# Dividing the attention features by their denominator ahead of one joined product

## The chip, the cores and the metric

The kernel runs on one core of one Trainium2 chip. The metric is the device time of one execution in microseconds (us), lower is better. Its engines work side by side, each through its own queue in order: PE (TensorE, matrix products and transposes into PSUM), DVE (VectorE, elementwise work), ACT (ScalarE, functions of one operand), POOL (GpSimd), and SP (SyncE, which issues DMAs). They wait for one another through semaphores.

## The reference, cut to what matters

The model has four layers; the change is in the attention of the last one. It is a linear attention over the 4096 pixels of each of 4 images, with 128 channels in 8 heads of 16:

```python
def _L3_attn_ref(Q, Wq, bq, Wk, bk, Wv, bv, Wo, bo):
    q = (Q @ Wq + bq).reshape(bs, seq, N_HEADS, HEAD_DIM)
    k = (Q @ Wk + bk).reshape(bs, seq, N_HEADS, HEAD_DIM)
    v = (Q @ Wv + bv).reshape(bs, seq, N_HEADS, HEAD_DIM)
    phi_q = jax.nn.elu(q) + 1.0
    phi_k = jax.nn.elu(k) + 1.0
    KV = jnp.einsum('blhd,blhm->bhdm', phi_k, v)
    K_sum = phi_k.sum(axis=1)
    Z = 1.0 / (jnp.einsum('blhd,bhd->blh', phi_q, K_sum) + EPS)
    V_new = jnp.einsum('blhd,bhdm->blhm', phi_q, KV) * Z[..., None]
    out = V_new.reshape(bs, seq, N_HEADS * HEAD_DIM) @ Wo + bo
    return out
...
t = t + _L3_attn_ref(_ln_t(t), ...)
```

So for each pixel and head there is a vector of 16 features `phi_q`, a denominator (one number for the head), and a 16x16 matrix `KV` that is the same for all pixels of an image.

## The kernel before, in words

The four images stay in SBUF (`xs`, 128 channels by 4096 pixels each). `layer3_attention` goes over them in chunks of 512 pixels, 8 to an image. For each image there are two generators.

`summed(b)` has three steps to a chunk: `norm` (the layer norm: a centring product `ln_xc`, squares on ACT, their mean by a product `ln_var`, a transpose `ln_vt` and an addition `ln_sd` on DVE, the power -1/2 on POOL (L140), four transposes on PE (L129) that spread the result, and the product `nrm` on DVE), `keys` (the joined product `kv` with the key and value matrices, then the key's feature `e_k`), and `add`, which accumulates `kv_sum` over all pixels in one PSUM tile by four products per chunk. At the end of the image, DVE turns `kv_sum` into `kvh` (the matrix `KV` of all heads, zero outside the 16x16 blocks, by the mask `same16`) and `ksh` (the sums of the features, masked alike).

`answered(b)` has three steps to a chunk as well: `queries` (the product `q_ps`, and its feature `e_q` through ACT and DVE), `weighed` (the products `den_ps` with `ksh` and `num_ps` with `kvh`; `den_t`, `rd`, `z`: the denominator is turned by 32x32 blocks, cut to one column per head, inverted, turned back and spread over the head; then `vn`, numerator times inverse), and `give` (the product `o_ps` with the output projection `wo`, and the addition to the image, `x` in the profile).

`in_turn` staggers the steps of one generator, so that in one turn step three works on chunk c, step two on c+1 and step one on c+2. `run` takes two generators in turns: the sums of image b+1 go along with the answers of image b. So the layer has three stages: the sums of image 0 alone, three times sums and answers together (8 chunks each), and the answers of image 3 alone.

The order of the instructions in each engine's queue isn't written out in the code: the framework orders them when the kernel is built, from the program order and its own estimate of when each could start. So an edit of one step can move others in the queues. All products here take fp32 operands, and one product shows as two records in the trace. PSUM tiles of the tag "mm" rotate through 7 buffers; most SBUF work tiles have 2.

Of the kernel before, what the change touches and what calls it, by code (L numbers as in the profile page):

```python
# [9 lines left out]
F32 = mybir.dt.float32  # L10
# [3 lines left out]
ALU = mybir.AluOpType  # L14
# [3 lines left out]
P = 128  # L18
# [3 lines left out]
CH = 512  # L22
# [8 lines left out]
class Common:  # L31
# [59 lines left out]
    def mm(self, out, lhsT, rhs, start=True, stop=True):  # L91
        self.nc.tensor.matmul(out, lhsT, rhs, start=start, stop=stop)  # L92
# [165 lines left out]
def column(nc, pool, v, name, n=1, p=P):  # L258

    t = pool.tile([p, n], F32, name=name)  # L260
    nc.sync.dma_start(out=t, in_=v.rearrange("(n p) -> p n", p=p))
    return t


def matrix(nc, pool, m, name, k=1):

    rows, f = m.shape
    if k == 1:
        t = pool.tile([rows, f], F32, name=name)
        nc.sync.dma_start(out=t, in_=m)  # L270
    else:
        t = pool.tile([rows // k, k, f], F32, name=name)
        nc.sync.dma_start(out=t, in_=m.rearrange("(k p) f -> p k f", k=k))
    return t


def rows(nc, pool, v, name):

    t = pool.tile([P, v.shape[0]], F32, name=name)
    nc.sync.dma_start(out=t, in_=v.partition_broadcast(P))  # L280
    return t
# [812 lines left out]
def in_turn(n, *stages):  # L1094


    for i in range(n + len(stages) - 1):
        for k in reversed(range(len(stages))):
            if 0 <= i - k < n:
                stages[k](i - k)  # L1100
                yield
# [21 lines left out]
def run(*parts):  # L1123
    for _ in in_turns(*parts):
        pass
# [875 lines left out]
def layer3_attention(K, xs, w):  # L2001

    nc, tc, mm = K.nc, K.tc, K.mm
    HD = 16
    with ExitStack() as ctx:
        pool = lambda name, bufs, **kw: ctx.enter_context(tc.tile_pool(reuse_waits="tile", name=name, bufs=bufs, **kw))
        cst = pool("l3_const", 1)
        big = pool("l3_big", 2)
        work = pool("l3_work", 2)
        psum = pool("l3_ps", 7, space=PSUM)  # L2010
        pskv = pool("l3_pskv", 1, space=PSUM)

        wkv = cst.tile([P, 2 * P], F32, name="wkv")
        nc.sync.dma_start(out=wkv[:, 0:P], in_=w["Wk"])
        nc.sync.dma_start(out=wkv[:, P : 2 * P], in_=w["Wv"])
        wq = matrix(nc, cst, w["Wq"], "wq")
        wo = matrix(nc, cst, w["Wo"], "wo")
        bk1 = rows(nc, cst, w["bk"], "bk")
        nc.vector.tensor_scalar(bk1, bk1, 1.0, None, ALU.add)
        bv = rows(nc, cst, w["bv"], "bv")  # L2020
        bq = column(nc, cst, w["bq"], "bq")
        bq1 = cst.tile([P, 1], F32, name="bq1")
        nc.vector.tensor_scalar(bq1, bq, 1.0, None, ALU.add)
        bo = column(nc, cst, w["bo"], "bo")
        less1 = cst.tile([P, 1], F32, name="less1")
        nc.vector.memset(less1, -1.0)

        vs = [cst.tile([P, 4, P + 1], F32, name=f"v{i}") for i in range(3)]
        for v in vs:
            nc.gpsimd.memset(v[:, :, P : P + 1], 1.0)  # L2030

        def feature(out, e, k1):

            nc.vector.scalar_tensor_tensor(out, e, 1.0, k1, ALU.min, ALU.max)

        kept = {}

        def summed(b):

            nrm = big.tile([P, L], F32, name="nrm")  # L2040
            kvp = pskv.tile([P, P + 1], F32, name="kv_sum")
            phis = {}

            def norm(c):
                cols = slice(c * CH, (c + 1) * CH)
                K.layernorm(nrm[:, cols], xs[b][:, cols], work, psum)

            def keys(c):

                k1 = work.tile([P, 4, P], F32, name="k1")  # L2050
                v = vs[(b * NCH + c) % 3]
                for i in range(2):
                    kv = psum.tile([P, 2, 2 * P], F32, name="kv", tag="mm")
                    for j in range(2):
                        at = c * CH + (2 * i + j) * P
                        mm(kv[:, j, :], nrm[:, at : at + P], wkv)
                    nc.vector.tensor_tensor(
                        k1[:, 2 * i : 2 * i + 2],
                        kv[:, :, 0:P],
                        bk1.unsqueeze(1).to_broadcast([P, 2, P]),  # L2060
                        ALU.add,
                    )
                    nc.scalar.copy(v[:, 2 * i : 2 * i + 2, 0:P], kv[:, :, P : 2 * P])
                e = work.tile([P, 4, P], F32, name="e_k")
                nc.scalar.activation(e, k1, AF.Exp, bias=less1)
                feature(e, e, k1)
                phis[c] = e, v

            def add(c):
                ph, v = phis.pop(c)  # L2070
                for j in range(4):
                    t = 4 * c + j
                    mm(kvp, ph[:, j, :], v[:, j, :], start=t == 0, stop=t == NTT - 1)

            yield from in_turn(NCH, norm, keys, add)

            kss = work.tile([P, 1], F32, name="kss")
            nc.vector.tensor_copy(kss, kvp[:, P : P + 1])
            kvh = work.tile([P, P], F32, name="kvh")
            nc.vector.scalar_tensor_tensor(kvh, bv, kss, kvp[:, 0:P], ALU.mult, ALU.add)  # L2080
            nc.vector.tensor_tensor(kvh, kvh, K.same16, ALU.mult)
            ksh = work.tile([P, P], F32, name="ksh")
            nc.vector.tensor_scalar(ksh, K.same16, kss, None, ALU.mult)
            kept[b] = nrm, kvh, ksh

        def answered(b):
            nrm, kvh, ksh = kept.pop(b)
            phis, vns = {}, {}

            def queries(c):  # L2090
                qp = psum.tile([P, CH], F32, name="q_ps", tag="mm")
                mm(qp, wq, nrm[:, c * CH : (c + 1) * CH])
                q1 = work.tile([P, CH], F32, name="q1")
                nc.scalar.activation(q1, qp, AF.Identity, bias=bq1)
                e = phis[c] = work.tile([P, CH], F32, name="e_q")
                nc.scalar.activation(e, qp, AF.Exp, bias=bq)
                feature(e, e, q1)

            def weighed(c):

                ph = phis.pop(c)
                dp = psum.tile([P, CH], F32, name="den_ps", tag="mm")
                mm(dp, ksh, ph)
                np_ = psum.tile([P, CH], F32, name="num_ps", tag="mm")
                mm(np_, kvh, ph)
                dt = work.tile([P, CH // 32, 2, HD], F32, name="den_t")
                nc.vector.transpose(dt.rearrange("p a h d -> p (a h d)"), dp)
                rd = work.tile([P, CH // 32, 2, 1], F32, name="rd")
                nc.vector.tensor_scalar(rd, dt[:, :, :, 0:1], 1e-5, None, ALU.add)
                nc.vector.reciprocal(rd, rd)  # L2110
                z = work.tile([P, CH // 32, 2, HD], F32, name="z")
                nc.vector.transpose(z, rd.to_broadcast([P, CH // 32, 2, HD]))
                vn = vns[c] = work.tile([P, CH], F32, name="vn")
                nc.vector.tensor_tensor(vn, z.rearrange("p a h d -> p (a h d)"), np_, ALU.mult)

            def give(c):
                op = psum.tile([P, CH], F32, name="o_ps", tag="mm")
                mm(op, wo, vns.pop(c))
                at = xs[b][:, c * CH : (c + 1) * CH]
                nc.vector.scalar_tensor_tensor(at, op, bo, at, ALU.add, ALU.add)  # L2120

            return in_turn(NCH, queries, weighed, give)

        run(summed(0))
        for b in range(NB):
            run(*([summed(b + 1)] if b + 1 < NB else []), answered(b))
# [81 lines left out]
```

## Time and profile before

| | |
|---|---|
| runs | 9564.62, 9565.78, 9581.03 us (median 9565.78) |
| profiled execution | 9578.96 us, span 9577.2 us |
| PE busy | 8608.8 us (90%) |
| DVE busy | 7159.3 us (75%) |
| ACT busy | 7287.0 us (76%) |
| POOL busy | 4933.0 us (52%) |
| mean granted clock of PE | 0.934 |
| third layer's attention in the span | about 8941 to 9295 us |

A row of the timeline has the start in us from the beginning of the span, the duration, the engine, the line, the operation, the tiles (out<-in) and shapes, and in brackets how long the engine had been idle and which instruction ended the wait. PEld is PE's weight load. A row of busy times by stretch has the busy us of each engine, with the number of its instructions in parentheses, and the clock that PE was granted (1.00 is full, 0.50 half).

### The profile page before, as it was taken

To read this page: it belongs to the slowest core of one execution; us is meant where nothing else is said; L and a number is where in the kernel's file an instruction comes from. 1 tells how busy PE (TensorE), PEld (TensorE's weight loads), DVE (VectorE), ACT (ScalarE), POOL (GpSimd) and SP (SyncE) were. 2 spreads that over 40 slices of the span, in tenths; PEclk is the share of its full clock that TensorE was granted. 3 is DMA by queue.
4 is the path that set the end of the run, shared out by engine and by line. 5 is a ranking of instruction groups with operands and counts; after the bars stand their busy time and mean duration, and the time that the engine had idled before them with its cause. 6 is when DMAs were issued, how large, how long until landed. Compare 5 with 4: busy or idle time off the path is not lost.

```text
span 9577.2 us, 189161 instructions
## 1 busy us (share of the span) xinstructions
PE 8608.8 (90%) x74394; PEld 3287.8 (34%) x74394; DVE 7159.3 (75%) x7845; ACT 7287.0 (76%) x10505; POOL 4933.0 (52%) x3287
## 2 busy tenths in 40 slices
PE   5887888889879999979999979999989999998787
PEld 2221222234443333333333333333333333334444
DVE  1889798987858888868888867888876888874464
ACT  3776767654449999969999969999978999984232
POOL 1677676765525555555555545555555555543011
PEclk8887888889989999989999989999989999999998
DMA  4434425222232221141222233221222222231205
GB/s 118 122 77 109 108 72 128 74 67 80 71 86 39 39 41 40 32 112 40 40 40 40 39 94 55 38 41 39 39 81 62 40 40 40 40 97 58 81 10 168
DMA packets 580323, 631.22 MB, mean 66 GB/s; under 512 B 118816, under 2 KB 374888, under 8 KB 578536
## 3 DMA queue, kind: packets, MB, share of 16 engines
q1 hardware_dynamic: 579432, 619.12, 27.5%
q8 instruction: 586, 9.60, 0.4%
q14 instruction: 305, 2.50, 0.1%
HBM read 444.74 MB, written 106.97 MB: 58 GB/s over the span
## 4 chain that ended last, share of the span: by engine, by line
PE 60%; DVE 4%; DMA 2%; POOL 2%; issue 2%; ACT 2%; SPq 0%; DVEq 0%; POOLq 0%; ACTq 0%
PE ctx_ps L92 27%; PE acc_ps L92 14%; PE score L92 12%; PE ln_xc L92 1%; DMA w<-in_L_ffn_weight 1%; PE hid_ps L92 1%; PE kv L92 1%; POOL ln_sd L1845 1%; PE ln_var L129 1%; DVE ctx L1498 0%; DMA queries<-head_d 0%; POOL q L1293 0%; PE pool L92 0%; DVE x L1998 0%; ACT hid L1685 0%
## 5 line engine op out<-in xcount | busy, mean ns | idle before, releaser
L1564 ACT ACTIVATE ex<-score 128x1024 f32<-128x1024 f32 x5120 | 4924.1, 1038 | 235.8 <-PE score L92 147.9
L92 PE MATMUL ctx_ps<-ex,qt 128*32 128x512 f32 x20480 | 2733.2, 606 | 19.7 <-DVE ctx L1498 19.7
L1513 POOL TENSOR_TENSOR folded<-ex 128x1024 f32<-128x1024 f32 x512 | 1223.3, 2389 | 2100.3 <-ACT ex L1564 1826.9
L1570 DVE STREAM_TRANSPOSE turned<-ex 128x1024 f32<-128x1024 f32 x1536 | 1885.3, 1227 | 337.1 <-ACT ex L1564 336.8
L1546 DVE STREAM_TRANSPOSE turned<-ex 128x1024 f32<-128x1024 f32 x1532 | 1841.9, 1202 | 0.0
L92 PE MATMUL acc_ps<-turned,turned_v 128*32 128x256 f32 x24576 | 1769.3, 379 | 3.0 <-POOL qt L1251 2.3
L926 DVE TENSOR_TENSOR_SCAN hs<-decay,carry,hs 128x512 f32<-128x512 f32 x1024 | 1245.4, 1265 | 196.9 <-ACT decay L922 183.8
L92 PE MATMUL score<-queries,keys 32*128 32x512 f32 x10240 | 1334.3, 497 | 51.9 <-POOL queries L1241 47.0
L92 PEld LDWEIGHTS acc_ps<-turned,turned_v 128*32 128x32 f32 x24576 | 800.8, 110 | 1476.6 <-issue 1324.4
L930 POOL TENSOR_TENSOR hs<-hs,c_sb 128x1024 f32<-128x1024 f32 x512 | 1207.0, 2357 | 70.4 <-DMA c_sb<-c_d 31.4
L922 ACT ACTIVATE decay<-dt,a_neg 128x512 f32<-128x512 f32 x1024 | 693.0, 689 | 659.8 <-DVE hs L926 649.8
L92 PEld LDWEIGHTS score<-queries,keys 32*128 32x128 f32 x10240 | 512.4, 182 | 1145.7 <-ACT ex L1564 777.7
L1370 POOL TENSOR_TENSOR turned_v<-v,quarter 128x1024 f32<-128x1024 f32 x256 | 612.9, 2395 | 264.8 <-PE acc_ps L92 222.5
L92 PE MATMUL y_ps<-hs,pair 128*64 128x512 f32 x2048 | 656.1, 769 | 32.2 <-POOL hs L930 32.2
L1514 POOL TENSOR_TENSOR quarters<-folded 128x512 f32<-128x512 f32 x512 | 657.6, 1284 | 40.1
L92 PEld LDWEIGHTS ctx_ps<-ex,qt 128*32 128x32 f32 x20480 | 406.4, 108 | 655.2 <-issue 599.1
L915 DVE TENSOR_TENSOR hs<-dtx,b_ps 128x2048 f32<-128x2048 f32 x256 | 579.8, 2265 | 54.9 <-PE b_ps L92 31.0
L92 PE MATMUL b_ps<-dbc,state 32*64 32x512 f32 x1024 | 340.8, 747 | 237.4 <-DVE hs L915 237.3
L929 POOL COPY carry<-hs 128x2 f32<-128x2 f32 x512 | 97.9, 191 | 688.3 <-DVE hs L926 659.6
L1564 ACT ACTIVATION_READ_ACCUMULATOR ex<-score 128x1 f32 x2048 | 439.0, 214 | 0.0
L1498 DVE COPY ctx<-ctx_ps 128x512 f32<-128x512 f32 x256 | 176.8, 691 | 329.3 <-PE ctx_ps L92 317.8
L1555 DVE TENSOR_REDUCE dacc<-quarters 128x2 f32<-128x512 f32 x508 | 326.9, 643 | 0.0
(376 smaller groups left out, 8785.0 us busy)
## 6 DMA issues: line engine op xcount, KB each, us to landing
c_sb<-c_d SPq DMA_DIRECT2D x512, 128.0 KB
keys<-head_d SPq DMA_DIRECT2D x1024, 64.0 KB
queries<-head_d SPq DMA_DIRECT2D x1024, 64.0 KB
under<-image_d SPq DMA_DIRECT2D x192, 264.0 KB
dt<-dt SPq DMA_DIRECT2D x128, 256.0 KB
dtx<-dtx SPq DMA_DIRECT2D x128, 256.0 KB
v<-value_d SPq DMA_DIRECT2D x1024, 32.0 KB
w<-in_L_ffn_weight SPq DMA_DIRECT2D x32, 1024.0 KB
```

What stands on the lines that cost most here:

```text
L92: self.nc.tensor.matmul(out, lhsT, rhs, start=start, stop=stop)
L915: nc.vector.tensor_tensor(hs, dtx2, bb.unsqueeze(1).to_broadcast([P, NQ, CH]), ALU.mult)
L922: nc.scalar.activation(ex, dt2[:, q, :], AF.Exp, scale=a_neg[:, q, g : g + 1])
L926: nc.vector.tensor_tensor_scan(hs[:, q, :], decays[q - 2 * i], hs[:, q, :], carry[:, g, q : q + 1], ALU.mult, ALU.add)
L930: nc.gpsimd.tensor_tensor(hs[:, two, :], hs[:, two, :], cs.unsqueeze(1).to_broadcast([P, 2, CH]), ALU.mult)
L1370: nc.gpsimd.tensor_tensor(t, v.unsqueeze(2).to_broadcast([P, 4 * BT, 4, HD]), quarter.unsqueeze(1).to_broadcast([P, 4 * BT, 4, HD]), ALU.mult,
L1513: nc.gpsimd.tensor_tensor(hs, exs[:, :, 0], exs[:, :, 1], ALU.add)
L1514: nc.gpsimd.tensor_tensor(qs, hs[:, :, 0 : CH // 2], hs[:, :, CH // 2 :], ALU.add)
L1546: nc.vector.transpose(*upright)
L1555: nc.vector.tensor_reduce(at, qs, AX.X, ALU.add)
L1564: nc.scalar.activation(ex, sps[p], AF.Exp, scale=scale, accum_out=sums[:, t : t + 1] if summed else None)
L1570: nc.vector.transpose(*upright)
```

## The change

Before, each chunk's features went through two products, one with `ksh` for the denominator and one with `kvh` for the numerator; the numerator was divided and then multiplied by `wo`. Now the features themselves are multiplied by the inverse denominator of their head, and then go through a single product with the matrix `kvo`, which is `kvh` times `wo`. It is made once per image: a transpose of `kvh` on PE, a copy from PSUM, a product with `wo`, and a copy. The `num_ps` product of each chunk goes.

```diff
             ksh = work.tile([P, P], F32, name="ksh")
             nc.vector.tensor_scalar(ksh, K.same16, kss, None, ALU.mult)
-            kept[b] = nrm, kvh, ksh
+            tp = psum.tile([P, P], F32, name="kv_t", tag="mm")
+            nc.tensor.transpose(tp, kvh, K.ident)
+            kvt = work.tile([P, P], F32, name="kvt")
+            nc.vector.tensor_copy(kvt, tp)
+            both = psum.tile([P, P], F32, name="kvo_ps", tag="mm")
+            mm(both, kvt, wo)
+            kvo = work.tile([P, P], F32, name="kvo")
+            nc.vector.tensor_copy(kvo, both)
+            kept[b] = nrm, kvo, ksh
...
                 mm(dp, ksh, ph)
-                np_ = psum.tile([P, CH], F32, name="num_ps", tag="mm")
-                mm(np_, kvh, ph)
...
-                nc.vector.tensor_tensor(vn, z.rearrange("p a h d -> p (a h d)"), np_, ALU.mult)
+                nc.vector.tensor_tensor(vn, z.rearrange("p a h d -> p (a h d)"), ph, ALU.mult)
...
-                mm(op, wo, vns.pop(c))
+                mm(op, kvo, vns.pop(c))
```

More of the change, by code (lines that the diff above doesn't have):

```diff
@@ L2083, in summed @@
             nc.vector.tensor_scalar(ksh, K.same16, kss, None, ALU.mult)
-            kept[b] = nrm, kvh, ksh
+            tp = psum.tile([P, P], F32, name="kv_t", tag="mm")
[7 more added lines that the diff above has]
+            kept[b] = nrm, kvo, ksh
         def answered(b):
-            nrm, kvh, ksh = kept.pop(b)
+            nrm, kvo, ksh = kept.pop(b)
             phis, vns = {}, {}
```

## The prediction

> Forecast: 9586 us, about 20 us (0.2%) slower. That is at the edge of what can be measured: a difference under 0.2% (19 us) can hardly be told from no change here, as the three runs shown span 16 us themselves.
>
> **What bounds the kernel now.** I cut the span by stage first. The third layer's attention has three stages: the sums of image 0 alone, three images' sums together with the answers of the image before ("joint"), and the last image's answers alone ("solo"). Columns: stretch and length in us; busy us (instructions) of PE, PE's weight loads, DVE, ACT and POOL; granted clock, DMA share, GB/s.
>
> ```profile
> 8941.00:9014.00 73.00, 49.07 (x247) 31.82 (x248) 22.47 (x52) 21.17 (x43) 8.06 (x8) 0.86 0.00 0
> 9014.00:9248.00 234.00, 202.40 (x907) 114.85 (x906) 156.33 (x324) 88.09 (x166) 24.15 (x24) 1.00 0.00 1
> 9248.00:9295.00 47.00, 34.06 (x69) 12.75 (x70) 34.19 (x61) 10.12 (x16) 0.04 (x1) 0.95 0.07 23
> ```
>
> The whole layer is 354 of 9577 us, so nothing done here can be worth much more than the removed product. PE is busiest in the joint stage (86%), but a busy share doesn't say that PE ends the chunk. For that I read the timeline of one joint chunk, from one `kv` product (9097.00) to the next (9106.44): 9.44 us.
>
> ```profile
> 9097.00 1.99 PE L92 MATMUL kv<-wkv,nrm 128*128 128x256 f32 x8 [0.85 <-DVE nrm L131]
> ...
> 9098.84 1.02 PE L92 MATMUL den_ps<-e_q,ksh 128*128 128x512 f32 x2
> 9099.69 1.02 PE L92 MATMUL num_ps<-e_q,kvh 128*128 128x512 f32 x2
> 9100.53 0.68 DVE L2034 SCALAR_TENSOR_TENSOR e_k<-e_k,k 128x512 f32<-128x512 f32 x1
> 9100.55 1.02 PE L92 MATMUL ln_xc<-x,center 128*128 128x512 f32 x2
> 9102.55 0.69 DVE L2114 TENSOR_TENSOR vn<-z,num_ps 128x512 f32<-128x512 f32 x1
> 9103.15 0.31 DVE L120 STREAM_TRANSPOSE ln_vt<-ln_var 128x128 f32<-128x128 f32 x1
> 9103.88 1.01 POOL L140 TENSOR_TENSOR ln_sd<-ln_sd,minus_half 128x4 f32<-128x4 f32 x1 [8.43 <-PE q_ps L92]
> 9104.86 0.75 DVE L2120 SCALAR_TENSOR_TENSOR x<-o_ps,bo,x 128x512 f32<-128x512 f32 x1 [1.13 <-PE o_ps L92]
> 9105.70 0.69 DVE L131 TENSOR_TENSOR nrm<-ln_kept,ln_var 128x512 f32<-128x512 f32 x1
> 9106.44 1.99 PE L92 MATMUL kv<-wkv,nrm 128*128 128x256 f32 x8 [0.85 <-DVE nrm L131]
> ```
>
> `kv` waits for `nrm`, the layer norm of the next chunk. Its chain runs over PE, DVE (`ln_vt` stands in DVE's queue behind `vn`), POOL and PE again. So a ring through several queues sets the chunk, not PE's work alone. A 128x512 product holds PE for 0.86 us (9098.84 to 9099.69), and its reader starts 1.06 us after it does.
>
> In the solo stage:
>
> ```profile
> 9282.86 0.30 PEld L92 LDWEIGHTS o_ps<-vn,wo 128*128 128x128 f32 x2 [2.06 <-DVE vn L2114]
> ...
> 9283.83 1.02 PE L92 MATMUL den_ps<-e_q,ksh 128*128 128x512 f32 x2
> 9284.69 1.02 PE L92 MATMUL num_ps<-e_q,kvh 128*128 128x512 f32 x2
> 9284.89 0.72 DVE L2107 STREAM_TRANSPOSE den_t<-den_ps 128x512 f32<-128x512 f32 x1
> 9287.06 0.69 DVE L2114 TENSOR_TENSOR vn<-z,num_ps 128x512 f32<-128x512 f32 x1
> 9287.80 0.30 PEld L92 LDWEIGHTS o_ps<-vn,wo 128*128 128x128 f32 x2 [2.06 <-DVE vn L2114]
> ```
>
> The ring is `o_ps`, `den_ps`, DVE's steps to `vn`, `o_ps`: 4.94 us. The product `num_ps` lies beside DVE's steps.
>
> **The change, part by part.** It removes 32 `num_ps` products (0.86 us of PE each, 27.5 us in all); `vn` multiplies by the feature in SBUF, at no other price (the same operation on two SBUF tiles, at L1886, has a median of 679 ns; `vn` takes 687); and per image it adds a transpose, two 128x128 copies and a product. The built order of the queues also changes, and that decides.
>
> *Joint chunk.* Zero is `kv`'s start; before's stamps are those shown, less 9097.00. New PE order: `kv`, `den_ps`, `ln_xc`, one product of `kv_sum` (before: three), `ln_var`, `q_ps`, three of `kv_sum`, `o_ps`. New DVE order: `z`, `ln_vt`, `vn`, `ln_sd`, the next `e_q`, `x`, `nrm` (before: `z`, `vn`, `ln_vt`, `ln_sd`, `x`, `nrm`, `e_q`).
> - `ln_xc` starts at 2.69 instead of 3.55. But the `kv_sum` product behind it waits for `e_k`, which DVE ends at 4.21; load and product (0.33) end at 4.59. PE idles there for 0.7 of the 0.86 saved.
> - `ln_var` at 4.59 (before 5.26), `q_ps` at 4.95 (before 5.62). DVE: `z` ends at 5.44 as before, `ln_vt` at 5.36, `vn` at 5.59, `ln_sd` ends at 6.36. POOL 6.50 to 7.51, 0.38 earlier. The transposes' result is due at 8.32, not 8.70.
> - `nrm` now stands behind `e_q` and `x`. `q_ps` is read by ACT 1.22 after its start (6.17), ACT's `e_q` ends at 7.44, DVE's `e_q` starts at 7.48, `x` 0.60 later, `nrm` 0.67 after that: 8.75 against 8.70 before. The 0.38 is given back.
>
> So `kv` follows at about 9.49. My rounding of hand-overs is worth 0.08, so 9.41 to 9.49; I take 9.44, no change, with ±1 us over 21 such chunks. If `e_q` weren't ahead, it would be -0.38 x 21 = -8.
>
> *Between images.* The added product must follow the sums, and its steps block both queues.
> - Twice inside the joint stage (`kv` at 9084.22, next at 9097.00): `o_ps` starts at 9090.48 and `ln_xc` right behind it, 9091.45. Now `kv_t` and `kvo_ps` stand between them, and the copy `kvt` stands behind `x` on DVE: `x` at 9091.65, +0.67 = 9092.32, copy 0.29 (row L1972: 128x128 from PSUM, 291 ns), `kvo_ps` 0.05+0.33, so `ln_xc` at 9092.99: +1.5 each, +3.1. Behind it wait `ln_var`, `q_ps` and all of the next chunk.
> - After image 0, `ln_xc` of image 1 ran at 9010.35, before the sums. Now it waits for them: `e_k` ends at 9012.72, sums 1.20, `kss` to masked `kvh` 0.90, transposed and copied 0.76, `kvo_ps` 0.38: `ln_xc` at 9016.01. From an uncovered `ln_xc` to `kv` it is 5.55 (9091.45 to 9097.00), so `kv` at 9021.56 instead of 9018.17: +3.4.
> - Into the solo stage `q_ps` slips likewise from 9249.12 by 1.5.
>
> *Solo chunk* at full clock: 0, `num_ps` isn't in the ring. Sum so far: 0 + 3.1 + 3.4 + 1.5 = **+8**.
>
> *The clock.* In the solo stage `num_ps` also kept PE busy. The granted clock changes in steps of 3.41 us:
>
> ```profile
> 9249.03:9252.44 3.41, 1.18 (x4) 0.28 (x2) 1.44 (x2) 1.26 (x2) 0.00 (x0) 1.00 0.00 0
> 9252.44:9255.86 3.42, 3.42 (x5) 1.34 (x6) 1.49 (x4) 0.00 (x0) 0.00 (x0) 0.52 0.02 5
> 9279.75:9283.16 3.41, 2.17 (x6) 0.87 (x5) 2.94 (x7) 1.26 (x2) 0.00 (x0) 1.00 0.00 0
> ```
>
> A window with PE busy for 1.18 us was followed by one at half clock; 2.17, the solo stage's lowest, wasn't. I tallied all 2797 such windows of the span. At full clock: PE busy under 1.5 us, 90 of 98 were followed by half clock; 1.5 to 1.9, 33 of 43; above, 20 of 2288. At half clock: under 2.9 us, 1 of 164 was followed by full clock; above, 141 of 203. The Trainium skill ("TensorE: Matmul & The Clock Gate", "Why this matters for your kernels") asks only that PE have no idle gaps over some 3 us; the gap here grows from 1.24 to 2.10 us a chunk, so by the rule the clock holds and the sum stays +8. By the windows it doesn't: one that holds the whole gap has 3.41-2.10 = 1.31 us busy. A window sliding over a 4.94 us chunk holds over 1.9 of the gap in 34% of positions and 1.5 to 1.9 in 16%, so full clock is left in 0.34x0.92 + 0.16x0.77 = 44% of windows. At half clock `o_ps` and `den_ps` add 0.97 + 0.86: the chunk is 6.77, PE busy 5.51 of it, 46% of windows hold over 2.9, and 0.46x0.69 = 32% return. Half clock then holds 0.44/0.76 = 58% of the stage, more as it is entered at half clock (as before). Ends: 0, and 7 chunks x 1.83 = +12.8. I take +8, two thirds of the upper end, as the windows are this kernel's own.
>
> The holes between images do the same. After image 0 PE has about 1.2 us of work from 9011.0 to 9014.4: half clock under `ln_xc`, `ln_var`, the transposes and `kv`, +2.5 (0 to +4). The two joint holes reach some 1.8 us, at the edge: +2 together (0 to +4). Steady joint chunks lose 0.7 us of cover around `e_k`, but apart from the 0.85 us hole before `kv`; their lowest window was 2.44, so I leave their clock at 1.00.
>
> Sum: +8 + 8 + 2.5 + 2 = **+20.5**. The profiled execution took 9578.96 us (span 9577.2), 13 above the median of 9565.78; its extra time isn't what the change touches, so the difference is added to the median: 9586.
>
> Downstream, the next layer's small weight loads no longer wait for the last `o_ps` (before, SP sat from 9287.6 to 9294.09), but those weights are first used after 9411: nothing.
>
> **Rivals.**
> - *The clock holds* (the page's rule): +8, 9574. For it: gaps of 2.10 us are below its 3. Against: the tally.
> - *PE is the bound* and the ring closes sooner: 21 x 0.86 = -18, with +8 between images: 9556. For it: 86% busy. It ends on the other side, and decides if DVE's `e_q` and `x` don't hold `nrm`, that is if `nrm` starts before 8.3 in its chunk. Against: PE has 0.7 us of new idle time behind `ln_xc`.
> - *Half clock reaches the joint chunks* through the new 0.7 us hole: a slow window costs about 1.7 us; 8 of the joint stage's 69 would give +14: 9600.
>
> **How the numbers follow.** Likeliest 0.50 (own range 9578 to 9596), clock holds 0.32, PE bound 0.08, joint half clock 0.10. Of the likeliest, 0.44 lies above 9584.9; with the last case slower is 0.54. PE bound is faster by over 0.2% in 0.05. The rest, 0.41, is within. Range 9566 to 9602: all but the PE-bound case and the outer tails.
>
> **What would show it.** Right: joint chunks within 0.1 of 9.44, PE idle behind `ln_xc`, `x` immediately ahead of `nrm`; about 14.3 us between `kv` products at the two joint changes of image, about 13 at the first; granted clock well below 0.95 in the solo stage and chunks there of 5 to 6.8 us. Wrong: joint chunks of 9.0 or less, or a solo stage at full clock.

## The result

The changed kernel takes 9603.74 us (median of 6 runs, 9588.39 to 9620.54) against 9570.28 us for the kernel before (6 runs, 9560.02 to 9581.03). The ratio is 1.0031, with a 95% interval of 1.002 to 1.0042: slower by about 30 us, where +20.5 was forecast. The profiled execution took 9602.94 us, with a span of 9601.2.

In the two profiled executions all of it lies in the third layer's attention. From its first `ln_xc` to its last addition to the image it took 353.84 us before and 383.97 after, +30.1; what precedes the layer was 4.5 us shorter after the change, and what follows it took 282.4 and 280.8.

The profile after, in the stretches that were shown of before (length; busy us and instructions of PE, weight loads, DVE, ACT and POOL; granted clock, DMA share, GB/s):

```profile
8941.00:9014.00 73.00, 48.75 (x235) 31.28 (x233) 22.94 (x54) 19.25 (x39) 7.05 (x7) 0.85 0.00 0
9014.00:9248.00 234.00, 184.88 (x810) 104.46 (x810) 137.94 (x300) 84.18 (x158) 23.16 (x23) 0.92 0.00 1
9248.00:9310.00 62.00, 42.17 (x105) 18.46 (x105) 39.09 (x75) 13.95 (x24) 1.01 (x1) 0.81 0.00 0
```

The clock changed too: from 1.00 to 0.92 in the joint stage and from 0.95 to 0.81 in the solo stage. PE's busy time in the joint stage fell by 17.5 us, and the layer became longer all the same. (The stage boundaries shift by some us after the change, so lengths are taken from instruction to instruction below.)

One steady joint chunk of the kernel after, from the timeline, between `kv` at 9050.10 and the next at 9059.66:

```profile
9050.10 1.99 PE L92 MATMUL kv<-wkv,nrm 128*128 128x256 f32 x8 [1.41 <-DVE nrm L131]
9051.93 1.02 PE L92 MATMUL den_ps<-e_q,ksh 128*128 128x512 f32 x2
9052.79 1.02 PE L92 MATMUL ln_xc<-x,center 128*128 128x512 f32 x2
9054.36 0.49 PE L92 MATMUL kv_sum<-v,e_k 128*128 128x129 f32 x2 [0.55 <-DVE e_k L2034]
9054.78 0.42 PE L92 MATMUL ln_var<-ln_sq,mean 128*32 128x128 f32 x8
...
9057.66 0.69 DVE L2034 SCALAR_TENSOR_TENSOR e_q<-e_q,q 128x512 f32<-128x512 f32 x1 [1.27 <-ACT e_q L2104]
9058.27 0.74 DVE L2126 SCALAR_TENSOR_TENSOR x<-o_ps,bo,x 128x512 f32<-128x512 f32 x1
9058.93 0.68 DVE L131 TENSOR_TENSOR nrm<-ln_kept,ln_var 128x512 f32<-128x512 f32 x1
```

9.56 us, where it was 9.44. PE's new idle time behind `ln_xc` is there (0.55 us ahead of `kv_sum`), and `x` runs immediately ahead of `nrm`, so that `nrm` waits for DVE's queue: `e_q`, `x`, `nrm` start one after the other, 0.6 to 0.7 us apart, from the moment ACT hands over its `e_q`. The product that went isn't in this ring.

A change of image in the joint stage looks like this (timeline, kernel after):

```profile
9092.89 1.16 PE L92 MATMUL kv_sum<-v,e_k 128*128 128x129 f32 x8 [1.41 <-DVE e_k L2034]
9094.90 1.68 PE L92 MATMUL o_ps<-vn,kvo 128*128 128x512 f32 x2 [0.85 <-DVE vn L2120]
9096.37 0.42 PE L2085 MATMUL kv_t<-ident,kvh 128*128 128x128 f32 x1
9096.61 0.75 DVE L2126 SCALAR_TENSOR_TENSOR x<-o_ps,bo,x 128x512 f32<-128x512 f32 x1 [1.11 <-PE o_ps L92]
9097.28 0.28 DVE L2087 COPY kvt<-kv_t 128x128 f32<-128x128 f32 x1
9097.62 0.79 PE L92 MATMUL kvo_ps<-wo,kvt 128*128 128x128 f32 x2 [0.83 <-DVE kvt L2087]
9098.20 1.92 PE L92 MATMUL ln_xc<-x,center 128*128 128x512 f32 x2
...
9103.38 1.11 PE L129 MATMUL ln_var<-ident,ln_sd 128*128 128x128 f32 x4
```

The order is the one forecast: `kv_t`, `x`, `kvt`, `kvo_ps`, and only then `ln_xc`. But `ln_xc` takes 1.92 us instead of 1.02, and `kvo_ps` 0.79 where it takes 0.49 in runs at full clock: half clock. The wait of 1.41 us ahead of `kv_sum` is where `num_ps` lay; before, PE waited 0.55 us there:

```profile
9088.48 1.16 PE L92 MATMUL kv_sum<-v,e_k 128*128 128x129 f32 x8 [0.55 <-DVE e_k L2034]
```

The clock windows around the change, kernel after:

```profile
9088.53:9091.94 3.41, 2.85 (x10) 1.82 (x10) 1.31 (x4) 1.20 (x3) 0.00 (x0) 1.00 0.02 5
9091.94:9095.36 3.42, 1.62 (x9) 1.27 (x10) 3.33 (x10) 0.17 (x1) 0.00 (x0) 1.00 0.00 0
9095.36:9098.77 3.41, 2.58 (x6) 1.12 (x5) 1.38 (x4) 0.00 (x0) 0.00 (x0) 0.50 0.00 0
9098.77:9102.18 3.41, 2.66 (x11) 0.70 (x10) 0.49 (x2) 1.08 (x2) 0.00 (x0) 0.50 0.00 0
9102.18:9105.59 3.41, 2.56 (x7) 0.96 (x6) 0.99 (x2) 1.27 (x2) 1.01 (x1) 0.50 0.00 0
9105.59:9109.01 3.42, 3.42 (x9) 2.70 (x10) 0.73 (x2) 0.38 (x1) 0.00 (x0) 0.50 0.00 0
9109.01:9112.42 3.41, 2.86 (x16) 1.23 (x15) 2.75 (x6) 2.08 (x4) 0.00 (x0) 1.00 0.00 0
```

One window with PE busy for 1.62 us (the second) is followed by four at half clock. That window ends at 9095.36, before `kv_t` starts: at this change the missing product emptied it, not the new matrix. In three of the four PE is busy for 2.56 to 2.66 us, which doesn't bring the clock back; it comes back after one that is busy from end to end. This happens at each of the three changes of image, four windows each (at the first, the window ahead of them holds 1.16 us: `ln_xc` of image 1, which ran there before, now waits for the matrix). At the first change one more stands a window ahead of them, under the last `kv` of image 0. The kernel before has such a window too, but 8.5 us ahead of that `kv`, so that it falls in the stage of image 0. The first row is of the kernel before (that `kv` starts at 9008.52), the second of the kernel after (9002.83):

```profile
8999.99:9003.40 3.41, 3.41 (x9) 2.31 (x7) 0.85 (x2) 0.57 (x2) 0.00 (x0) 0.50 0.00 0
9003.18:9006.60 3.42, 3.13 (x8) 1.97 (x6) 0.67 (x2) 0.37 (x1) 0.00 (x0) 0.50 0.00 0
```

Solo stage, two windows that held a chunk's gap (`den_ps` to `o_ps`, 2.1 us), each with the window after it:

```profile
9296.74:9300.15 3.41, 1.29 (x4) 0.44 (x3) 3.17 (x7) 1.27 (x2) 0.00 (x0) 1.00 0.00 0
9300.15:9303.57 3.42, 3.42 (x5) 1.34 (x5) 1.03 (x3) 0.00 (x0) 0.00 (x0) 0.50 0.00 0
9303.57:9306.98 3.41, 1.38 (x3) 0.34 (x3) 3.23 (x6) 1.27 (x2) 0.00 (x0) 1.00 0.00 0
9306.98:9310.39 3.41, 3.41 (x5) 1.35 (x4) 1.35 (x2) 0.00 (x0) 0.00 (x0) 0.50 0.00 0
```

From one `o_ps` to the next it took 6.67, 4.97, 4.94, 4.93, 6.55, 6.26 and 4.84 us: those at full clock keep the old 4.94, the others pay.

### The profile page after: what moved, and what is told of

It reads as the page before. It is cut to its first block, busy times and chain, and to the rows that moved or that the text cites. A ratio compares the mean times of both kernels' runs of the same rounds, so it can differ in the third digit from the quotient of the medians.

```text
span 9601.2 us, 189041 instructions
## 1 busy us (share of the span) xinstructions
PE 8603.4 (90%) x74342; PEld 3283.6 (34%) x74342; DVE 7155.6 (75%) x7853; ACT 7291.3 (76%) x10505; POOL 4933.7 (51%) x3287
## 4 chain that ended last, share of the span: by engine, by line
PE 59%; DVE 4%; DMA 2%; POOL 2%; ACT 2%; issue 2%; SPq 1%; DVEq 0%; POOLq 0%; ACTq 0%
PE ctx_ps L92 27%; PE acc_ps L92 14%; PE score L92 12%; DMA w<-in_L_ffn_weight 1%; PE ln_xc L92 1%; PE kv L92 1%; PE hid_ps L92 1%; POOL ln_sd L1845 1%; DMA keys<-head_d 1%; DMA queries<-head_d 0%; PE ln_var L129 0%; DVE ctx L1498 0%; POOL q L1293 0%; PE pool L92 0%; DVE x L1998 0%
## 5 line engine op out<-in xcount | busy, mean ns | idle before, releaser
L92 PE MATMUL y_ps<-hs,pair 128*64 128x512 f32 x2048 | 654.4, 767 | 31.3 <-POOL hs L930 31.3
```

## The experiments

Two theories were set against each other. A: most of the loss comes from making the joined matrix at each change of image. B: most of it comes from the product that is gone, which had kept PE busy. Later runs split the loss into work that lies on the path and half clock, and then try to get it back. Each ratio is against the kernel before on the same chip. As runs scatter by 20 to 30 us, the trace of each kernel's profiled execution is used beside the ratio. It was cut from `kv` to `kv`; "from the first change" is the time from the last `kv` of image 0 to the end of the layer (before 286.3 us, after 317.6: +31.3).

**chain_only: the matrix is made and not used.**

```diff
             nc.vector.tensor_scalar(ksh, K.same16, kss, None, ALU.mult)
+            tp = psum.tile([P, P], F32, name="kv_t", tag="mm")
+            nc.tensor.transpose(tp, kvh, K.ident)
...
+            kvo = work.tile([P, P], F32, name="kvo")
+            nc.vector.tensor_copy(kvo, both)
             kept[b] = nrm, kvh, ksh
```

> The kernel before, with the joined matrix made for each image as in the change and then not used; the chunks keep both products. Theory A (the price is paid between images: the steps that make the matrix block PE and DVE, and the holes drop PE to half clock): +20 to +25 us, the three joint changes of image some 16 us from kv to kv as in the changed kernel, half clock after each, chunks inside an image 9.44. Theory B (the price is the removed product: reordered chunks and an emptier PE): 0 to +3 us.

Measured: 1.0015 (1.0008 to 1.0022), 9590.01 against 9576.30 us. From the first change 300.5 us, +14.2. Changes of image took 15.62, 14.32 and 14.32 us (before 9.65, 12.78, 12.78), the chunk after each of the last two 11.10 instead of 9.44, steady chunks 9.44. Three windows were at half clock at the first change and one behind each of the others. So making the matrix, with the half clock that it brings, costs about half of the loss: less than A had said, and more than B.

**no_num: the product goes and no matrix is made.** This kernel leaves out the product with the matrix `KV`: `vn` is the feature times the inverse denominator, and goes straight into `wo`.

```diff
-                np_ = psum.tile([P, CH], F32, name="num_ps", tag="mm")
-                mm(np_, kvh, ph)
...
-                nc.vector.tensor_tensor(vn, z.rearrange("p a h d -> p (a h d)"), np_, ALU.mult)
+                nc.vector.tensor_tensor(vn, z.rearrange("p a h d -> p (a h d)"), ph, ALU.mult)
```

> The kernel before without the numerator product and without the joined matrix: the features over the denominator go straight to the output projection, so the product with the matrix of keys and values is left out. Theory A: +4 to +9 us, joint chunks 9.56, changes of image within 0.5 us of before (12.8), half clock only in parts of the solo stage. Theory B: +22 to +30 us. If PE were the bound of the joint chunks: -15 us or less.

Measured: 1.0010 (1.0003 to 1.0016), 9589.04 against 9576.30 us. From the first change 300.5 us, +14.2. Steady chunks took 9.56, the changes 11.69, 14.22 and 12.79, and from the last `kv` to the end 59.45 instead of 52.95. So a kernel with less work and nothing added is slower than the kernel before, by about 10 us by the ratio. Of the 14.2 us in the trace, 6.5 are the solo stage and 2.4 the steady chunks; 3.8 stand at the first change and the chunk behind it, at least 2.0 of them because half clock from the stage of image 0 ran on into the change in this execution. Neither theory holds alone. The two traces add up to 28.4 of 31.3, but with one execution each the difference of 2.9 is no measure of what the two parts do to each other. The second change shows that they do something. The clock windows of no_num there:

```profile
9095.93:9099.34 3.41, 1.58 (x9) 1.26 (x10) 3.32 (x10) 0.20 (x1) 0.00 (x0) 1.00 0.00 0
9099.34:9102.75 3.41, 3.00 (x4) 0.67 (x2) 0.93 (x2) 0.32 (x1) 0.00 (x0) 0.50 0.00 0
9102.75:9106.17 3.42, 2.13 (x14) 0.87 (x14) 0.53 (x3) 2.03 (x4) 1.01 (x1) 1.00 0.00 0
```

The clock falls behind the same hole as in the changed kernel (1.58 us busy, there 1.62), but it is back after one window: with no matrix to make, `ln_xc` follows `o_ps` at once and PE is busy for 3.00 us. In the changed kernel `kv_t`, the copy and `kvo_ps` stand between them, that window holds 2.58 us, and three more follow at half clock. The missing product loses the clock here, and the steps of the matrix keep it from coming back.

**late_kvo: the change, with the matrix made at its first use**, in `weighed` of the first chunk, away from the head of the next image's chain. The same four steps stand in a function `join`; the cut is against the changed kernel.

```diff
-            kept[b] = nrm, kvo, ksh
+            kept[b] = nrm, kvh, ksh
...
                 mm(dp, ksh, ph)
+                if c == 0:
+                    join()
...
-                mm(op, kvo, vns.pop(c))
+                mm(op, joined[0], vns.pop(c))
```

> The changed kernel with the joined matrix made later, in the step that weighs the image's first chunk, just ahead of its first use; nothing is left out. Theory A: changes of image go back to about 13 us plus at most 1 us in the chunk after, no half clock there, and the total is within 3 us of the kernel without the matrix: +5 to +10. Theory B: no better than the change, +25 to +30.

Measured: 1.0020 (1.0013 to 1.0026), 9590.84 against 9576.30 us. From the first change 300.3 us, +14.0. The first change is free again (9.66) and the third nearly (12.79); the second had 14.24. The chunk after each costs 10.59. What stays is the steady chunk of 9.56 and the solo stage of 59.72. The place of the matrix is worth about 17 us in the trace; by the ratios (1.0031 and 1.0020) it is some 10, and their intervals touch. Moving it doesn't bring the kernel back to the old time.

**warm_all: the change with filler products**, whose results nobody reads: in `add` of each image's last chunk (two for image 0, one for the others), one between the copy `kvt` and `kvo_ps`, and in the solo stage one for each chunk in the place of `num_ps`. 17 in all: 9 at the changes, 8 in the solo stage.

```diff
+                if c == NCH - 1:
+                    warm(2 if b == 0 else 1)
...
             nc.vector.tensor_copy(kvt, tp)
+            warm(1)
...
                 mm(dp, ksh, ph)
+                if b + 1 == NB:
+                    np_ = psum.tile([P, CH], F32, name="num_ps", tag="mm")
+                    mm(np_, ksh, ph)
```

> The changed kernel with filler products whose results nobody reads: one or two in PE's waits at each change of image, and one in each solo chunk where the numerator product was. Nothing is left out, PE has 16 products more. If half clock is the larger part of the loss: granted clock 1.00 from the first change of image on, changes of 11.5 to 14.5 us, +9 to +14 us in total against the kernel before. If the clock is only a symptom and the queues' waits alone make the loss: +30 us or more, since the fillers add to them.

Measured: 1.0013 (1.0006 to 1.0019), 9590.47 against 9576.30 us. From the first change 299.7 us, 17.9 less than the change. Busy time by stretch in warm_all, from the last `kv` ahead of the second change to 9.50 us behind the first `kv` after it, and from the last `kv` to the end of the layer:

```profile
9082.07:9105.90 23.83, 18.04 (x79) 9.70 (x79) 13.88 (x32) 7.44 (x14) 2.02 (x2) 1.00 0.00 0
9244.56:9299.66 55.10, 41.37 (x94) 16.71 (x95) 38.71 (x71) 11.50 (x19) 0.00 (x0) 0.95 0.14 41
```

The same two stretches of the kernel after:

```profile
9088.63:9114.85 26.22, 20.98 (x73) 11.11 (x74) 12.10 (x30) 7.44 (x14) 2.01 (x2) 0.74 0.00 1
9259.53:9320.44 60.91, 39.83 (x74) 16.02 (x75) 38.26 (x71) 11.50 (x19) 0.00 (x0) 0.78 0.13 38
```

More products, and the clock rises from 0.74 to 1.00 at the change and from 0.78 to 0.95 in the solo stage; both stretches are shorter. With a full clock the second and third change took 14.33 and 14.32 us. So at least 18 of the 31 us are half clock. The other 13 stay with the clock nearly held (at the changes one half-clock window is left in this run, the one under the last `kv` of image 0; the solo stage has one at its entry): steps on the path.

**warm_change: the same without the fillers of the solo stage.**

```diff
+                if c == NCH - 1:
+                    warm(2 if b == 0 else 1)
...
             nc.vector.tensor_copy(kvt, tp)
+            warm(1)
```

> The changed kernel with fillers at the changes of image alone; the solo stage has none. Nothing is left out. By the traces so far half clock costs 12 us at the changes and 6 us in the solo stage: this kernel should be 10 to 12 us faster than the changed one, so +16 to +22 against before, with solo chunks of 6.5 us again. By the working of the prediction, 4.5 at the changes and 8 in the solo stage: +25 against before.

Measured: 1.0015 (1.0009 to 1.0022), 9592.25 against 9577.39 us; from the first change 301.9 us. The solo part took 57.31 at a clock of 0.86, against 60.91 at 0.78 after and 55.10 at 0.95 with all fillers: it is entered at a better clock, and has half clock again later. The split of the prediction, 8 us for the solo stage and 4.5 for the changes, would have left about +25 here; the fillers at the changes alone took away 15.7 in the trace, 3.6 of it in the solo part. By the ratio this run and warm_all (1.0013) can't be told apart, so what the solo fillers add rests on the traces. The first change ran wholly at full clock in this run, in 13.33 us; in warm_all it took 14.97, with one window at half clock under its `kv`.

**late_warm: late_kvo with the solo fillers alone.**

```diff
                 mm(dp, ksh, ph)
+                if b + 1 == NB:
+                    np_ = psum.tile([P, CH], F32, name="num_ps", tag="mm")
+                    mm(np_, ksh, ph)
```

> The kernel with the joined matrix made late, and one filler product in each solo chunk where the numerator product was, its result unread. Nothing is left out. If the solo stage loses by the clock alone: last kv to the end 52.9 to 54 us as before the change (59.7 without filler), -6 us against the kernel with the late matrix, +5 to +11 against before. If something else in the solo stage costs: still 58 us or more.

Measured: 1.0010 (1.0001 to 1.0018), 9587.98 against 9577.39 us. The solo part took 56.24 us instead of 59.72, not the 52.9 to 54 expected: the stage is still entered at half clock, and the fillers hold a clock that they find, but don't bring it back at once. From the first change it was 302.9 us, no better than late_kvo: the third change took 14.85 and the chunk after it 13.02 in this execution, with three windows at half clock, and the edit touches neither.

**late_order: late_kvo, with the query's feature kept behind the norm in DVE's queue.**

```diff
-            nc.vector.tensor_tensor(out, kept, vp, ALU.mult)
+            self.last_norm = nc.vector.tensor_tensor(out, kept, vp, ALU.mult)
...
-                feature(e, e, q1)
+                with tc.issue_after(K.last_norm.ins):
+                    feature(e, e, q1)
```

> The kernel with the joined matrix made late, and one more edge in the built order: the query feature's DVE step of a chunk is queued behind the layer norm's last step of the same turn. Nothing is left out. If that step ahead of the norm is what gives the saving back: joint chunks 9.05 to 9.15 instead of 9.56, 20 of them, so -9 us against the kernel with the late matrix, and 0 to +8 against before. If the order doesn't matter (PE's wait for the key feature or the POOL step sets the chunk): 9.45 to 9.56, and +12 to +20 against before.

Measured: 1.0009 (1.0001 to 1.0017), 9588.15 against 9577.39 us. Steady joint chunks take 9.13 us, 0.43 less than with the change and 0.31 less than before, and the joint stage keeps its full clock in the steady chunks. That is the removed product's gain, and the only place where one was found. In the profiled execution the stage of image 0 alone, which the edit doesn't touch, ran at half clock (72.9 us instead of some 61, as it did in no_num), so only the part from the first change is used: 294.2 us, +7.9. Even that begins at half clock: the first change took 11.71 and the chunk after it 12.27, where late_kvo has 9.66 and 10.59.

**best: late_order with the solo fillers.** The cut is against late_order.

```diff
+                if b + 1 == NB:
+                    np_ = psum.tile([P, CH], F32, name="num_ps", tag="mm")
+                    mm(np_, ksh, ph)
```

> Both together: late matrix, query feature queued behind the norm, filler in the solo chunks; nothing is left out. Savings of the two should add: joint chunks 9.1, solo stage 53, chunks after a change of image +1 us each: -7 + 3 = -4 us against before, between -10 and +3. If the emptier PE now drops to half clock inside the joint stage: +5 us or more.

Measured: 0.9997 (0.9989 to 1.0005), 9574.23 against 9577.39 us: no difference from the kernel before. From the first change 288.9 us. The timeline of DVE in a joint chunk of this kernel shows the order:

```profile
9061.47 0.75 DVE L2135 SCALAR_TENSOR_TENSOR x<-o_ps,bo,x 128x512 f32<-128x512 f32 x1 [1.44 <-PE o_ps L92]
9062.14 0.68 DVE L131 TENSOR_TENSOR nrm<-ln_kept,ln_var 128x512 f32<-128x512 f32 x1
9062.73 0.69 DVE L2034 SCALAR_TENSOR_TENSOR e_q<-e_q,q 128x512 f32<-128x512 f32 x1
```

The steady chunks give 18 x 0.31 = 5.6 us back, but the first change (11.29), the chunks after the changes (10.59 to 10.95) and the entry to the solo stage (55.55 to the end, against 52.95) take 1.6, 3.8 and 2.6. The 1.6 is again a half-clock window under the last `kv` of image 0.

**best2: best with the two copies on ACT and three more fillers behind the first two query products of the solo stage** (two and one).

```diff
-                nc.vector.tensor_copy(kvt, tp)
+                nc.scalar.copy(kvt, tp)
...
+                if b + 1 == NB and c < 2:
+                    for _ in range(2 - c):
+                        wp = psum.tile([P, CH], F32, name="warm", tag="mm")
+                        mm(wp, wq, nrm[:, 0:CH])
```

> The last version (late matrix, query feature behind the norm, fillers in the solo chunks) with two more edits: the two copies of the joined matrix on ACT instead of DVE, and three fillers at the entry to the solo stage. Nothing is left out. If the 1.1 to 1.5 us that each first chunk after a change still loses come from DVE's copies in the ring: first chunks 9.2 to 9.6 instead of 10.6, solo stage 53 instead of 55.5, so -9 to -5 us against before. If they come from PE's products in the ring: 10.3 and more, and 0 to -3.

Measured: 1.0002 (0.9993 to 1.0011), 9575.49 against 9573.28 us. The expected gain didn't come: the solo part fell to 53.83 us, but the second and third change rose to 14.78 and 14.09, with half clock in both. The chunks after the changes took 11.02, 11.93 and 9.93; half clock lies in the first two, and the third is between the two forecasts, so they don't tell whether DVE's copies or PE's products cost the time. No version tried is measurably faster than the kernel before.

## Why the forecast was right, and by what

The direction and the mechanism hold, and 9603.74 less 9570.28 is 33 us (30 by the ratio), against +20.5 with a range that ended at +36. The time went to other places than the sum said, and that the total stayed within the range is in part luck: the clock at the changes cost more than the upper ends given for it (0 to +4 twice), and the solo stage less than was said. "At full clock" is from warm_all and warm_change.

| step of the prediction | said, us | measured, us | from |
|---|---|---|---|
| joint chunks | 0 | +2.8 | 9.56 instead of 9.44; one of 9.84 |
| first change, on the path | +3.4 | +3.7 | 13.33 - 9.65 at full clock |
| two joint changes, on the path | +3.1 | +3.1 | 14.33 and 14.32, less 12.78 each |
| entry to the solo stage | +1.5 | +2.2 | 55.10 - 52.95 at clock 0.95 |
| half clock, solo stage | +8 | +5.8 | 60.91 - 55.10 |
| half clock, first change | +2.5 | +5.3 | 16.60 + 11.55, less 13.33 + 9.50 |
| half clock, two joint changes | +2 | +8.4 | 16.72 + 11.34 and 16.83 + 11.24, less 14.33 + 9.56 each |
| sum | +20.5 | +31.3 | 317.6 - 286.3 |

The stage of image 0 alone, which the change leaves as it is, took 1.1 us less; that makes the +30.1 of the layer. It belongs together with the first change: of the 5.3 us of half clock there, about 1.6 is the window under the last `kv` of image 0 (14.97 us in warm_all with that window alone, 13.33 in warm_change without), and its like before the change counts to the stage of image 0. Without it the clock at the changes cost some 12 us.

- *Joint chunk.* The working was right in kind: what `ln_xc` gains is lost behind `e_k`, and `e_q` and `x` hold `nrm`. The size was off by one term: the product of `kv_sum` with its load was put at 0.33 us and takes 0.42 (9054.36 to 9054.78). That carries through `ln_var` (4.68 instead of 4.59), `q_ps` (5.04 for 4.95) and `nrm` (8.83 for 8.75) to `kv` at 9.56, just outside the 9.41 to 9.49 given and 0.02 over the "within 0.1 of 9.44". The conditional forecast beside it, 0.38 less if `e_q` weren't ahead, is borne out in kind by late_order: 9.13, 0.31 less than before.
- *Between images.* The times on the path were good to some tenths where the clock held: about 14.3 was said, 14.32 and 14.33 came; about 13 was said for the first, 13.33 came (the working's terms to 9016.01 add up to 9015.96; that changes nothing). In the changed kernel itself they are 16.7, 16.8 and 16.6, which is the next point.
- *The clock at the changes is the term that was mis-sized*: 4.5 us said, 13.7 in the table, some 12 without the window of image 0. The holes were seen rightly (about 1.2 us of work said for the first, 1.16 came; holes of 1.8 us said for the others, 3.41 - 1.62 came). At its own 1.7 us for a slow window, the prediction counted one or two windows for the first hole and about half of one for each of the others. The step that failed is this, with the bounds of 0 to 4 us for the first and for the other two together: it priced the falling of the clock and forgot the return. The prediction's own tally had it: at half clock, windows with PE busy under 2.9 us returned once in 164. At each change comes a chain with PE busy for 2.17 to 2.67 us per window, so three more windows stay at half clock, and the `kv` behind it ends the stretch with its full window. In no_num, where the window after the hole held 3.00 us, the clock was back at once.
- *The clock in the solo stage* was said at +8 and came at +5.8. Three chunks after the entry stayed at the full clock by the position of their windows (a gap window with 1.44 us busy kept it, those with 1.29 and 1.38 lost it).
- *The rival that the clock holds* (+8, by the Trainium skill, "TensorE: Matmul & The Clock Gate", "Why this matters for your kernels": no idle gaps over some 3 us) fell: no gap of PE in the solo stage exceeds 2.9 us, and the clock there was 0.78. If the clock had held, the loss would have been 11.8 us, the first four rows of the table.
- *PE as the bound* fell: the chunk didn't become shorter until DVE's order was changed as well. *Half clock in the steady joint chunks* fell too: windows away from the changes are at 1.00 (the chunk after a change belongs to the change).

What isn't settled: why best and best2 lose at the changes about what they win in the chunks. Their traces show half clock at some of the changes in one execution each. Which windows fall seems to depend on where the boundaries of the windows lie, and that wasn't controlled: in late_kvo the hole of the second change left 1.62 us in one window and a half-clock window followed; at the third, with the same instructions, the window held 1.90 us and none did. Each trace is one execution, and the stage of image 0 alone, which no edit is meant to touch, took 65.5 to 67.6 us from its first `ln_xc` to its last `kv` in nine of the eleven kernels and 80.0 and 80.1 in late_order and no_num, so differences of a few us between traces carry little. Not tried is best with the fillers at the changes, which would fill the hole ahead of `kv_sum` that best and best2 leave open.

## What to carry to other kernels

A product that lies beside other work on the busiest engine may be what keeps that engine's clock up: before taking it away, count how busy each 3.41-us window will be without it, and how busy those are from which the clock has to return. At the changes here the clock fell behind windows with some 1.6 us of work and less, and windows of 2.6 us did not bring it back. Price a hole by the whole stretch until PE is busy from end to end again, not by its own length. And where a ring of queues sets the chunk, find what stands ahead of the last step in its queue: here moving one DVE step behind `nrm` gave 0.43 us per chunk, where removing 0.86 us of PE work had given none by itself.

## What the hardware showed that was not expected

- Half clock lasts: one 3.41-us window with PE busy for 1.62 us led to four at half clock (13.7 us) although PE was busy for 75 to 78% of the first three of them. Since work at half clock takes longer, a chain of dependent small products looks busy and still doesn't bring the clock back.
- Work that nobody reads can shorten a kernel: 17 products added to the changed one took 17.9 us off the layer in the trace, counted from the first change, and the ratio from 1.0031 to 1.0013.
- Removing work alone, with nothing put in its place, made the kernel slower: 1.0010 (1.0003 to 1.0016).
